# Forming keys already turned, with their norm sent through DRAM, in a fused cross-attention kernel

## The chip, the cores and the metric

The kernel runs on one core of one Trainium2 chip. A core has five engines that run side by side: TensorE (PE; its weight loads are shown apart as PEld), VectorE (DVE), ScalarE (ACT), GpSimd (POOL) and SyncE (SP), which here issues the DMAs. TensorE writes to PSUM (eight banks of 512 float32 for each of 128 partitions); the other engines work on SBUF, and all but GpSimd on PSUM too. The metric is the device time of one execution in microseconds, as the median of several runs.

## What is computed

Eight sequences b of 64 tokens `x[b]` (512 features) attend to a context `ctx[b]` of 1601 rows of 512 features. The part that the change touches is the cross-attention; of the reference:

```python
kvx = jnp.einsum('bsi,oi->bso', cond, w_kv_x)
kx, vx = jnp.split(kvx, 2, axis=-1)
kx = _ln(kx.reshape(b, sc, g, d), kxln_w, kxln_b)      # g = 8 heads of d = 128
vx = vx.reshape(b, sc, g, d)
xout = _gqa(qx, kx, vx).reshape(b, s, nh * d)
...
scores = jnp.einsum('bsghd,btgd->bghst', q, k) * scale
p = jax.nn.softmax(scores, axis=-1)
```

`_ln` subtracts the mean over d, divides by the root of the variance plus 1e-5, then applies a weight and a bias. So each key of each head needs one number of its own, r = 1/sqrt(mean square + 1e-5); the mean is taken out of the weights beforehand (`key_weights`), so that only r is left to find. Around this stand a self-attention with fp8 rounding, an output projection, a sparse attention among the 64 tokens and a ternary feed-forward network. All products with large operands are made exact enough by splitting a float32 number into a high and a low float32r part (`hi`, `lo`) and adding three matmuls: hi x hi, lo x hi, hi x lo.

## The kernel before

**Tiling.** The 1601 context rows are 13 tiles of 128 (`TT`; the last has 65), and the tiles form six chunks (`CHUNKS`): five of 256 keys and one of 321, which is rounded up to 322. The 8 key heads are two halves of 4 (`HG`). There are 16 work items, one for each half and sequence (`Cross`), and so 208 steps of one tile each.

**Order of work.** The loop at the end of `tile_perceiver` runs over g. In each g it issues a piece of several stages at different distances, so that one work item's late stages run beside the next one's early ones: `keys` for tile g (L542), `keys_t` for tile g-1 (L567), `scores` for the chunk that ends at tile g-2 (L580), and, `LAG` = 17 steps behind, `probs_t`, `context` and `weigh` (L621, L653, L678). Everything else (projections, self-attention, feed-forward) comes from generators pumped at a set pace (`bgA`, `bgB`, `bgC`), with lower priority. The program text sets priorities; a scheduler orders each engine's instructions before the run, and on the chip each engine goes through its own in that order.

**Keys.** `keys` loads a tile of the transposed context (cTr, by SyncE, L546), splits it (ScalarE L549 makes cThi, GpSimd L550 makes cTlo), and does 12 matmuls (L555) with the context tile stationary and 512 columns of weights (4 heads) moving, so that the keys lie on partitions. ScalarE squares them into ksq (L560) and copies them to kn (L561), VectorE sums the squares (L562), GpSimd takes the power -1/2 (L173), and VectorE multiplies kn by it (L564). `keys_t` turns kn by four TensorE transposes (L219), and ScalarE (L577, kthi) and VectorE (L578, ktlo) evict the result in two parts.

**Scores.** `scores` does, for each head of a chunk, three matmuls of 256 or 322 columns (L598), two heads in one bank (one head for the last chunk), and VectorE evicts them into the S tile (L602), adding a column of zeros, and takes the maximum on the way. Later ScalarE applies exp (L618), TensorE transposes the probabilities (L630), ScalarE and VectorE split them (L640, L641: phi, plo), and 12 matmuls a tile (L693 to L695) add them up with the context rows (cr, chi, clo) in four banks `acc`.

**Buffers.** S has 7 buffers, cThi and cTlo two each of one tile, raw (cTr, cr and others) three. PSUM: three banks `m` (keys, turned keys, scores, probabilities), four `acc`, one `b`; before step `LAG` - 1 keys use `acc` banks. In the last steps a class `Late` borrows buffers of the main stage for the last token pair.

Of the kernel before, what the change touches and what calls it, by code (L numbers as in the profile page):

```python
# [21 lines left out]
P = 128  # L22
H = 512
NIC = 4
S = 64
# [11 lines left out]
KTW = 324  # L37
NCH = len(CHUNKS)
CHUNK_OF = {tt: ci for ci, ch in enumerate(CHUNKS) for tt in ch}
LAG = 17  # L40
ALL = 10 ** 6
AHEAD = 2000
SPLIT = 1
FFN_AT = 6
# [13 lines left out]
def tile_perceiver(ctx: ExitStack, tc: tile.TileContext, t: dict):  # L58
# [83 lines left out]
    class Late:  # L142
# [5 lines left out]
        def _main(tag, bufs, dt=F32):  # L148
# [6 lines left out]
        pd = _main("kf", 2)  # L155
        ps = staticmethod(lambda tag="b": kxp())

        AT = {"hT": (0, 0), "ps_": (0, 0), "qkv": (0, 256), "sim": (0, 448), "mask": (1, 0), "eq": (1, 64), "cum": (1, 128),
              "pmx": (1, 192), "psu": (1, 224), "aoT": (1, 256), "kvg": (2, 0), "pr": (2, 768), "sT": (2, 1152), "ao": (2, 1216)}

        def tile(self, tag, shape):
            if not self.held:
                self.held = [mp.tile([P, 512], F32, tag="cTlo", name=nm("late"), bufs=2) for _ in range(2)]
                self.held.append(mp.tile([P, HG * KTW], F32, tag="S", name=nm("late"), bufs=7))
            k, o = self.AT[tag]
            a = self.held[k][:shape[0], o:o + math.prod(shape[1:])]
            return a if len(shape) == 2 else a.rearrange("p (x y) -> p x y", x=shape[1])
# [62 lines left out]
    mhalf = ctile([P, 4], F32, "mhalf")  # L230
# [41 lines left out]
    wpd = [dtile([P, 2, H], F32, f"wpd{c}") for c in range(32)]  # L272
    clod = [dtile([SC, H], F32, f"clod{b}") for b in range(NB)]
# [19 lines left out]
    def projection(v_, blocks, js, first=None):  # L293
# [17 lines left out]
        for nb in blocks:  # L311
# [4 lines left out]
            else:  # L316
                ws = [mp.tile([P, NIC, 256], F32, tag="S", name=nm("ws"), bufs=7)]
# [173 lines left out]
    def key_weights(half):  # L491
        hi = mp.tile([P, NIC, 512], F32R, tag="wkhi", name=nm("wkhi"), bufs=1)
        lo = mp.tile([P, NIC, 512], F32R, tag="wklo", name=nm("wklo"), bufs=1)
        for ic in range(NIC):
            tag, bufs = ("kf", 2) if half == 0 and ic >= 2 else ("raw", 3)
# [13 lines left out]
    ksq = ctile([P, HG, D + 1], F32, "ksq")  # L509
    GP.memset(ksq[:, :, D:], EPS)  # L510
# [9 lines left out]
    class Cross:  # L520


        def __init__(self, b, half):
# [4 lines left out]
            self.kn = {}  # L528
# [13 lines left out]
        def keys(self, tt):  # L542

            t0, n = TT[tt]
            raw = mp.tile([P, NIC, P], F32, tag="raw", name=nm("cTr"), bufs=3)
            paced[0] = nc.sync.dma_start(raw[:, :, :n], t["ctxT"][self.b].rearrange("(c p) k -> p c k", p=P)[:, :, t0:t0 + n])  # L546
            chi = mp.tile([P, NIC, P], F32R, tag="cThi", name=nm("cThi"), bufs=2)
            clo = mp.tile([P, NIC, P], F32R, tag="cTlo", name=nm("cTlo"), bufs=2)
            A.copy(chi[:, :, :n], raw[:, :, :n])  # L549
            GP.tensor_tensor(clo[:, :, :n], raw[:, :, :n], chi[:, :, :n].bitcast(F32), ALU.subtract)  # L550
            ps = kxp()
            k = 0
            for st, mv in ((chi, self.wk[0]), (chi, self.wk[1]), (clo, self.wk[0])):
                for ic in range(NIC):
                    PE.matmul(ps[:n], lhsT=st[:, ic, :n], rhs=mv[:, ic, :], start=k == 0, stop=k == 11)  # L555
                    k += 1
            kn = mp.tile([P, 512], F32, tag="kn", name=nm("kn"), bufs=3)
            sq = ksq
            v = sm("kxv", HG)
            A.activation(sq[:n, :, :D], v3(ps[:n], HG), AF.Square, scale=1.0 / math.sqrt(D))  # L560
            A.copy(kn[:n], ps[:n])  # L561
            V.tensor_reduce(v[:n], sq[:n], AX.X, ALU.add)  # L562
            r = rsqrt(v[:n], n, HG, "rqk")
            pin[0] = V.tensor_tensor(v3(kn[:n], HG), v3(kn[:n], HG), r.unsqueeze(2).to_broadcast([n, HG, D]), ALU.mult)  # L564
            self.kn[tt] = kn

        def keys_t(self, tt):  # L567
# [3 lines left out]
            c0 = TT[CHUNKS[ci][0]][0]  # L571
# [584 lines left out]
    for g in range(NA + LAG + 3):  # L1156
# [8 lines left out]
        if g == NA + 3:  # L1165
            lane["late"] = mainp("late")
# [15 lines left out]
        if g < NA:  # L1182
            work[nA].keys(kA)
# [139 lines left out]
```

## Time and profile before

| what | value |
|---|---|
| times of three runs | 1986.89, 1992.36, 1997.09 us |
| median | 1992.36 us |
| span of the profiled execution | 1990.0 us |
| that execution's own time | not given by the profile apart from its span |
| instructions | 32306 |
| DMA traffic | 352.02 MB, mean 177 GB/s |
| DMA queue of SyncE, share of 16 engines | 55.5% |

The span runs from the first to the last instruction of the program in the profiled execution. The profile gives each engine's busy time, then the span in 40 slices, the DMA queues, the chain of work that ended last (followed back from the last instruction to whatever released it), and groups of instructions: line, engine, operation, tiles written and read, shapes, count, then busy us, mean ns of one, the engine's idle time before them, and who ended it. Matmuls overlap in the array, so that one lasts longer than the distance to the next. In the timeline a line is: start, length in us, engine, line, operation, tiles, shape, how many in a row.

### The profile page before, as it was taken

The page shows a single profiled execution, that of the slowest core. Times are in us where ns is not written, and L with a number is a line of the kernel's source. Part 1 is how long each engine was busy: PE and PEld are TensorE (multiplying, and loading weights), DVE is VectorE, ACT ScalarE, POOL GpSimd, SP SyncE. Part 2 cuts the span into 40 slices and gives each one's busy share as a digit, 9 for nine tenths or more (in the row PEclk, how much of TensorE's full clock was granted, in tenths as well). Part 3 has the DMA queues.
Part 4 walks back from the last instruction along what each step waited for, and adds up shares of the span by engine and source line. Part 5 has one row for each costly group of instructions (what it writes and reads, how often), then busy time and mean ns, then how long its engine had stood idle before and what let it go on. Part 6 is the DMA issues. An engine that isn't in the chain of part 4 may idle for free.

```text
span 1990.0 us, 32306 instructions
## 1 busy us (share of the span) xinstructions
PE 1923.4 (97%) x10709; PEld 1593.6 (80%) x10709; DVE 1377.2 (69%) x3423; ACT 1215.9 (61%) x2724; POOL 634.1 (32%) x600
## 2 busy tenths in 40 slices
PE   7899999999999999999999999999999999999998
PEld 5678888888888887887888788888877787886776
DVE  7768688677678676776775665756577665655665
ACT  6576667666676566655664545555675566566554
POOL 6343334333333333223332323222233333220132
PEclk9899999999999999999999999999999999999999
DMA  6345545466455654557776667656745543564425
GB/s 199 115 140 164 160 143 162 142 209 211 132 171 157 216 160 122 186 172 265 236 265 225 200 199 257 200 188 204 269 136 162 172 157 94 156 209 139 142 65 178
DMA packets 296503, 352.02 MB, mean 177 GB/s; under 512 B 30336, under 2 KB 191232, under 8 KB 296336
## 3 DMA queue, kind: packets, MB, share of 16 engines
q1 hardware_dynamic: 296336, 349.97, 55.5%
q8 instruction: 84, 1.38, 0.3%
q14 instruction: 83, 0.68, 0.1%
HBM read 283.94 MB, written 65.68 MB: 176 GB/s over the span
## 4 chain that ended last, share of the span: by engine, by line
PE 83%; DMA 7%; DVE 5%; issue 2%; ACT 1%; POOL 1%; SPq 0%; POOLq 0%; ACTq 0%; DVEq 0%
PE kx L555 26%; PE acc L693 8%; PE acc L694 8%; PE acc L695 8%; PE s L598 6%; PE pj L340 4%; PE pt L630 4%; PE kx L219 4%; DMA ws<-wpd 3%; PE xo L714 3%; PE pp L431 2%; PE p L822 1%; DMA wv<-in_wkv 1%; PE tr L372 1%; PE y L1073 1%
## 5 line engine op out<-in xcount | busy, mean ns | idle before, releaser
L550 POOL TENSOR_TENSOR cTlo<-cTr,cThi 128x512 fp32r<-128x512 f32 (+1 forms) x208 | 274.4, 1320 | 891.2 <-PE kx L555 618.1
L694 PE MATMUL acc<-plo,chi 128*128 128x512 f32 x768 | 310.3, 405 | 0.4 <-DVE plo L641 0.4
L695 PE MATMUL acc<-phi,clo 128*128 128x512 f32 x768 | 303.8, 397 | 0.0
L562 DVE TENSOR_REDUCE kxv<-ksq 128x4 f32<-128x516 f32 (+1 forms) x208 | 142.9, 687 | 223.0 <-ACT ksq L560 222.8
L173 POOL TENSOR_TENSOR rqk<-kxv,mhalf 128x4 f32<-128x4 f32 (+1 forms) x208 | 217.8, 1047 | 127.1 <-DVE kxv L562 109.5
L693 PE MATMUL acc<-phi,chi 128*128 128x512 f32 x768 | 246.7, 402 | 1.7 <-ACT chi L670 1.0
L555 PE MATMUL kx<-wkhi,cThi 128*128 128x512 f32 (+1 forms) x832 | 240.8, 411 | 7.0 <-ACT wkhi L501 2.3
L549 ACT CAST cThi<-cTr 128x512 fp32r<-128x512 f32 (+1 forms) x208 | 125.9, 606 | 182.1 <-PE kx L555 84.1
L555 PE MATMUL kx<-wklo,cThi 128*128 128x512 f32 (+1 forms) x832 | 230.4, 397 | 0.0
L555 PE MATMUL kx<-wkhi,cTlo 128*128 128x512 f32 (+1 forms) x832 | 229.4, 395 | 0.0
L577 ACT ACTIVATE kthi<-kx,cols 128x512 fp32r<-128x512 f32 (+1 forms) x208 | 140.8, 677 | 137.2 <-PE kx L219 135.6
L670 ACT CAST chi<-cr 128x512 fp32r<-128x512 f32 x192 | 119.1, 620 | 141.7 <-PE acc L694 130.5
L618 ACT ACTIVATE S<-S,cnm 128x256 f32<-128x256 f32 (+1 forms) x384 | 197.1, 522 | 7.0 <-DVE cnm L613 6.8
L578 DVE SCALAR_TENSOR_TENSOR ktlo<-kx,cols,kthi 128x512 fp32r<-128x512 f32 (+1 forms) x208 | 150.9, 726 | 60.7 <-ACT kthi L577 59.9
L555 PEld LDWEIGHTS kx<-wklo,cThi 128*128 128x128 f32 (+1 forms) x832 | 155.0, 187 | 41.2 <-issue 1.6
L555 PEld LDWEIGHTS kx<-wkhi,cTlo 128*128 128x128 f32 (+1 forms) x832 | 154.3, 186 | 41.3 <-issue 3.2
L555 PEld LDWEIGHTS kx<-wkhi,cThi 128*128 128x128 f32 (+1 forms) x832 | 147.5, 188 | 39.2 <-ACT wkhi L501 3.5
L564 DVE TENSOR_TENSOR kn<-kn,rqk 128x512 f32<-128x512 f32 (+1 forms) x208 | 149.4, 718 | 39.4 <-POOL rqk L173 36.3
L602 DVE CUSTOM_DVE_ANT_0 S<-s,zeros 128x256 f32<-128x256 f32 (+1 forms) x384 | 151.9, 429 | 33.1 <-PE s L598 32.2
L694 PEld LDWEIGHTS acc<-plo,chi 128*128 128x128 f32 x768 | 145.0, 189 | 26.4 <-issue 1.7
L693 PEld LDWEIGHTS acc<-phi,chi 128*128 128x128 f32 x768 | 139.9, 189 | 32.7 <-ACT chi L670 2.8
L695 PEld LDWEIGHTS acc<-phi,clo 128*128 128x128 f32 x768 | 144.6, 189 | 26.1 <-issue 1.6
(344 smaller groups left out, 3770.5 us busy)
## 6 DMA issues: line engine op xcount, KB each, us to landing
cTr<-in_ctxT SPq DMA_DIRECT2D x192, 256.0 KB
cr<-in_ctx SPq DMA_DIRECT2D x192, 256.0 KB
ws<-wpd SPq DMA_DIRECT2D x88, 512.0 KB
clod<-clo SPq DMA_DIRECT2D x96, 256.0 KB
clo<-clod SPq DMA_DIRECT2D x96, 256.0 KB
wv<-in_wkv SPq DMA_DIRECT2D x64, 256.0 KB
tern<-in_ffn_w SPq DMA_DIRECT2D x64, 256.0 KB
wpd<-ws SPq DMA_DIRECT2D x32, 512.0 KB
```

Source lines behind the costliest of these rows:

```text
L173: GP.tensor_tensor(y[:n], v, mhalf[:n, :k], ALU.pow)
L550: GP.tensor_tensor(clo[:, :, :n], raw[:, :, :n], chi[:, :, :n].bitcast(F32), ALU.subtract)
L555: PE.matmul(ps[:n], lhsT=st[:, ic, :n], rhs=mv[:, ic, :], start=k == 0, stop=k == 11)
L562: V.tensor_reduce(v[:n], sq[:n], AX.X, ALU.add)
L564: pin[0] = V.tensor_tensor(v3(kn[:n], HG), v3(kn[:n], HG), r.unsqueeze(2).to_broadcast([n, HG, D]), ALU.mult)
L577: A.activation(hi[:, :, o], v3(pt, HG)[:, :, :n], AF.Copy, scale=hw["kx"])
L578: V.scalar_tensor_tensor(lo[:, :, o], v3(pt, HG)[:, :, :n], hw["kx"], hi[:, :, o].bitcast(F32), ALU.mult, ALU.subtract)
L602: V.tensor_tensor_reduce(sc[:, g, :cw], ps[:, :cw], zeros.to_broadcast([P, cw]), 1.0, -3.0e38, ALU.add, ALU.max, self.mx[:, g * NCH + ci:g ...
L618: A.activation(self.S[ci][:, g, :cw], self.S[ci][:, g, :cw], AF.Exp, bias=self.nmx[:, g:g + 1], accum_out=self.su[:, g * NCH + ci:g * NCH ...
L693: PE.matmul(self.U[ic], lhsT=chi[:n, s], rhs=phi[:n], start=tt == 0, stop=False)
L694: PE.matmul(self.U[ic], lhsT=chi[:n, s], rhs=plo[:n], start=False, stop=False)
L695: PE.matmul(self.U[ic], lhsT=clo[:n, s], rhs=phi[:n], start=False, stop=False)
```

## The change

Keys are now formed turned: the weights are stationary (128 columns of one head) and a whole chunk of the context moves (256 or 322 columns), so that a head's 128 features lie on partitions and keys along the free dimension, as scores need them. The four transposes of a tile, the copy kn, and the product with r before the transposes are gone. `keys` is split in two: `turned` loads and splits the context of a tile into buffers that hold a chunk (cThi, cTlo: two of 322 columns), and `keys` does two heads of a chunk (one head in the last chunk, whose four heads take three steps), evicting them unnormed.

The norm now runs over partitions. ScalarE's squares are turned by VectorE in 32x32 blocks, and summed over 32 columns (`ms`); `norm`, once a chunk, adds the four blocks of partitions by one TensorE product with a constant (`over`), picks each partition group's own head (`quad`), takes the power on GpSimd, turns the 32x32 blocks once more, writes 128 rows of 32 numbers to DRAM (`keyd`), and reads them back, broadcast to all 128 partitions, into the chunk's S tile. `scores` then multiplies by the S tile where it added zeros.

The stages move: context loads at step g, keys two steps later (`KEYS`), scores four steps after the load (`SCORES`; two before), `LAG` 19. S has 8 buffers (`SB`), taken at `norm`. `Late` moves its borrowed tiles to other tags.

```diff
-LAG = 17
+LAG = 19
+KEYS, SCORES = 2, 4
...
+SB = 8
...
+    quad = ctile([P, HG], F32, "quad")
+    for h in range(HG):
+        V.tensor_reduce(quad[:, h:h + 1], ident[:, h * 32:(h + 1) * 32], AX.X, ALU.add)
+    over = ctile([P, P], F32, "over")
+    for h in range(HG):
+        V.tensor_reduce(over[:, h * 32:(h + 1) * 32], ident.rearrange("p (q a) -> p a q", q=HG), AX.X, ALU.add)
+    spread = [ctile([P, 32], F32, f"spread{i}") for i in range(2)]
...
+    keyd = [[dtile([HG, 1024], F32, f"keyd{i}_{ci}") for ci in range(NCH)] for i in range(2)]
...
-        def keys(self, tt):
+        def turned(self, tt):
 
             t0, n = TT[tt]
+            ci = CHUNK_OF[tt]
+            o = t0 - TT[CHUNKS[ci][0]][0]
+            if ci not in self.ct:
+                self.ct[ci] = [mp.tile([P, NIC, CTW], F32R, tag=x, name=nm(x), bufs=2) for x in ("cThi", "cTlo")]
+            chi, clo = self.ct[ci]
             raw = mp.tile([P, NIC, P], F32, tag="raw", name=nm("cTr"), bufs=3)
...
+            A.copy(chi[:, :, o:o + n], raw[:, :, :n])
+            GP.tensor_tensor(clo[:, :, o:o + n], raw[:, :, :n], chi[:, :, o:o + n].bitcast(F32), ALU.subtract)
+
+        def keys(self, ci, gs):
...
+            ps = kxp()
+            for i, g in enumerate(gs):
+                k = 0
+                for st, mv in ((self.wk[0], chi), (self.wk[1], chi), (self.wk[0], clo)):
+                    for ic in range(NIC):
+                        PE.matmul(ps[:, i * N:(i + 1) * N], lhsT=st[:, ic, g * P:(g + 1) * P], rhs=mv[:, ic, :N], start=k == 0, stop=k == 11)
+                        k += 1
+            g0, g1, ng = gs[0], gs[-1] + 1, len(gs)
+            sq = mp.tile([P, 512], F32, tag="kn", name=nm("ksq"), bufs=3)
...
+            A.activation(v3(sq[:, :ng * W], ng)[:, :, :N], v3(ps[:, :ng * N], ng), AF.Square, scale=1.0 / math.sqrt(D))
+            A.activation(hi[:, g0:g1, :N], v3(ps[:, :ng * N], ng), AF.Copy, scale=hw["kx"])
+            sqt = mp.tile([P, 512], F32, tag="kn", name=nm("ksqt"), bufs=3)
+            V.transpose(sqt[:, :ng * W], sq[:, :ng * W])
+            V.scalar_tensor_tensor(lo[:, g0:g1, :N], v3(ps[:, :ng * N], ng), hw["kx"], hi[:, g0:g1, :N].bitcast(F32), ALU.mult, ALU.subtract)
+            pin[0] = V.tensor_reduce(self.ms[ci][:, g0 * nj:g1 * nj], sqt[:, :ng * W].rearrange("p (x a) -> p x a", a=32), AX.X, ALU.add)
...
+        def norm(self, ci):
+
+            cw = sum(TT[tt][1] for tt in CHUNKS[ci])
+            nj = (cw + 31) // 32
+            ms = self.ms.pop(ci)
+            z = mainp("kz")
+            PE.matmul(z[:, :HG * nj], lhsT=over, rhs=ms[:, :HG * nj], start=True, stop=True)
+            own = sm("kown", HG * NRM, bufs=1)
+            V.scalar_tensor_tensor(v3(own[:, :HG * nj], HG), v3(z[:, :HG * nj], HG), EPS, quad.unsqueeze(2).to_broadcast([P, HG, nj]), ALU.add, ALU.mult)
+            v = sm("kxv", NRM, bufs=2)
+            V.tensor_reduce(v[:, :nj], own[:, :HG * nj].rearrange("p (g j) -> p j g", g=HG), AX.X, ALU.add)
+            r = spread[ci % 2]
+            GP.tensor_tensor(r[:, :nj], v[:, :nj], mhalf[:, :nj], ALU.pow)
+            rt = sm("krt", 32, bufs=2)
+            V.transpose(rt, r)
+            rd = keyd[(self.b + self.half * NB) % 2][ci]
+            nc.sync.dma_start(rd.rearrange("g (x a) -> (g x) a", a=32), rt)
+            self.S[ci] = mp.tile([P, HG, KTW], F32, tag="S", name=nm("S"), bufs=SB)
+            load(self.S[ci][:, :, :cw], rd[:, :cw].partition_broadcast(P))
...
-                    V.tensor_tensor_reduce(sc[:, g, :cw], ps[:, :cw], zeros.to_broadcast([P, cw]), 1.0, -3.0e38,
-                                           ALU.add, ALU.max, self.mx[:, g * NCH + ci:g * NCH + ci + 1])
+                    V.tensor_tensor_reduce(sc[:, g, :cw], ps[:, :cw], sc[:, g, :cw], 1.0, -3.0e38,
+                                           ALU.mult, ALU.max, self.mx[:, g * NCH + ci:g * NCH + ci + 1])
...
+    TURN = {tt: (tt,) for tt in range(NT - 2)}
+    TURN[NT - 2] = NT - 2, NT - 1
+    JOBS = [(ci, [(2 * i, 2 * i + 1)]) for ci in range(NCH - 1) for i in range(2)]
+    JOBS += [(NCH - 1, x) for x in ([(0,)], [(1,)], [(2,), (3,)])]
...
         if g < NA:
-            work[nA].keys(kA)
+            for tt in TURN.get(kA, ()):
+                work[nA].turned(tt)
+        if 0 <= gK < NA:
+            ci, gs = JOBS[kK]
+            for x in gs:
+                work[nK].keys(ci, x)
+            if gs[-1][-1] == HG - 1:
+                work[nK].norm(ci)
...
-        if 0 <= g - 2 < NA:
-            nS, kS = divmod(g - 2, NT)
+        if 0 <= g - SCORES < NA:
+            nS, kS = divmod(g - SCORES, NT)
...
-        if 0 <= g - 1 < NA:
-            nT, kT = divmod(g - 1, NT)
-            work[nT].keys_t(kT)
```

## The prediction

> **What bounds the kernel now.** I read the page first (engines, slices, the chain that ended last), then TensorE in order of time, then the groups by line with shapes kept apart, then the waits. Two lines of the page:
>
> ```profile
> PE 1923.4 (97%) x10709; PEld 1593.6 (80%) x10709; DVE 1377.2 (69%) x3423; ACT 1215.9 (61%) x2724; POOL 634.1 (32%) x600
> ...
> PE kx L555 26%; PE acc L693 8%; PE acc L694 8%; PE acc L695 8%; PE s L598 6%; PE pj L340 4%; PE pt L630 4%; PE kx L219 4%; DMA ws<-wpd 3%; PE xo L714 3%; PE pp L431 2%; PE p L822 1%; DMA wv<-in_wkv 1%; PE tr L372 1%; PE y L1073 1%
> ```
>
> TensorE is busy nearly throughout and the chain's largest items are its matmuls: keys (L555) and key transposes (L219) are the ones that the change rewrites. A matmul's own duration is no price, since matmuls overlap. The price is start to start, which the timeline gives (start, length, instruction):
>
> ```profile
> 51.73 0.60 PE L219 MATMUL kx<-ident,kn 128*128 128x128 f32 x4
> 52.09 1.17 PE L555 MATMUL kx<-wkhi,cThi 128*128 128x512 f32 x4
> 53.09 1.07 PE L555 MATMUL kx<-wklo,cThi 128*128 128x512 f32 x4
> 54.00 1.08 PE L555 MATMUL kx<-wkhi,cTlo 128*128 128x512 f32 x4
> ...
> 73.42 3.00 PE L340 MATMUL pj<-ws,xq 128*128 128x256 f32 x23
> 76.25 1.09 PE L555 MATMUL kx<-wkhi,cThi 128*128 128x512 f32 x4
> ...
> 1026.83 1.09 PE L555 MATMUL kx<-wkhi,cThi 128*128 128x512 f32 x4
> ...
> 1029.56 0.39 PE L693 MATMUL acc<-phi,chi 128*128 128x512 f32 x1
> 1029.79 0.39 PE L598 MATMUL s<-kthi,qxhi 128*128 128x256 f32 x2
> ...
> 1030.49 0.63 PE L693 MATMUL acc<-phi,chi 128*128 128x512 f32 x2
> ```
>
> Read from it: a tile's 12 key matmuls take 1029.56 - 1026.83 = 2.73 us (0.2275 each); six score matmuls of 256 columns, each with weights of its own, take 0.70 (0.117 each); 23 of L340 take 2.83 (0.123). Four transposes take 0.36, and the four matmuls behind them 1.00 instead of 0.91: 0.45 in all.
>
> **TensorE, term by term.** Removed: 192 groups of four transposes x 0.45 = 86.4, and 16 of the one-row-over-64 tile, 0.24 each (1006.59 to 1006.83) = 3.8: **-90.2 us**. Rewritten: 208 x 2.73 = 567.8 becomes, for the 80 chunks of 256 keys, 80 x 48 matmuls of 256 columns, and for the 16 last chunks 16 x 48 of 322 columns. At 0.120, between the two 256-column rows, the first are 460.8 (449.3 at 0.117, 472.3 at 0.123). Three score matmuls of 322 columns start 0.45 apart in sum (1016.28 to 1016.73), so the second are 768 x 0.150 = 115.2. The last chunk gains, since its third tile of 65 keys no longer pays for 512 columns; the rest pays a little. Sum 576.0: **+8.2** (-3.3 to +19.7). Added: 96 small products z of 32 or 44 columns. Nearest: L463, 64 columns, 16 in 1.72 (1022.35 to 1024.07), 0.108 each: **+10.3** (9.6 at the 0.10 of L831's two columns, 22 at the 0.2275 of 512). TensorE together: -71.7.
>
> The Trainium skill speaks against narrower matmuls: "TensorE: Matmul & The Clock Gate", section "LDWEIGHTS (loading the stationary operand)", gives columns / 1.2 ns, so 107 ns for 128 columns whatever the matmul's width, and its section on the gap 256/2.4 + 2.5 = 109 ns; by both, 256 is about the narrowest width that hides the load. By its gap the keys would go from 539 to 524 us (an estimate from that page), -15 where I take +8; the rows above (0.117 to 0.123 and 0.2275) are slower than the page's and decide.
>
> **The other engines.** The groups that lose or change work:
>
> ```profile
> L564 DVE TENSOR_TENSOR kn<-kn,rqk 128x512 f32<-128x512 f32 x192 | 138.6, 722 | 37.1 <-POOL rqk L173 34.0 <-ACT fa L367 2.3
> L562 DVE TENSOR_REDUCE kxv<-ksq 128x4 f32<-128x516 f32 x192 | 132.0, 687 | 213.5 <-ACT ksq L560 213.3
> L602 DVE CUSTOM_DVE_ANT_0 S<-s,zeros 128x256 f32<-128x256 f32 x320 | 121.0, 417 | 15.6 <-PE s L598 14.8
> L561 ACT COPY kn<-kx 128x512 f32<-128x512 f32 x192 | 111.8, 582 | 0.0
> L173 POOL TENSOR_TENSOR rqk<-kxv,mhalf 128x4 f32<-128x4 f32 x192 | 200.5, 1044 | 102.4 <-DVE kxv L562 94.6 <-DVE cqb L605 5.1 <-DVE hag L356 1.0
> ```
>
> VectorE, per 256-key chunk: before 2 x (687 + 722 + 746 of L578) = 4.31 us. After: two turns by 32x32 blocks, two L578-like subtractions, two reductions, and in norm about 0.55 (L364's 217, L610's 160, a small turn). No row shows the turn. Nearest one-input rows of 128x512 are the copy L701 (682) and the reduction (687); I take 690 and keep 290 (L211, the fastest) to 890 (L473, the slowest) as ends. That is 4.8, +0.5 x 80; the last chunk goes from 6.16 to about 7.0, x 16: **+53 us**, 1430 of some 1922, 74%. Evicting scores by a product with the S tile is priced like L602, 417: L1006, also PSUM with SBUF at 256 columns, has 419.
> ScalarE loses 121 us (208 copies) and gains 3 in the last chunk's shapes: 57%. GpSimd loses 217.8; by L173's rows for 1, 2 and 4 columns (607, 700, 1044) a column costs 170 ns, so 80 pows of 8 columns (1.73) and 16 of 11 (2.24) add 174; memsets 10. All of this lies beside TensorE and is priced at nothing. If that cover went, VectorE's 53 is the price (95 with turns of 890, below nothing with turns of 290).
>
> **New waits.** z stands in TensorE's order behind a square, a turn and a reduction; behind it queue acc (L693-695) and scores, and everyone who evicts them. The key transposes waited for such a chain too (copy, reduction, pow, product) and cost 3.8 us of idle in 768; so 0 to 4 us, taken as no change. SyncE gets 192 DMAs: the read into the S tile waits until the write has landed, and for a free S tile (released by pt transposes a step earlier); behind it queue the loads of cTr, cr and clo, the casts, then acc. VectorE's score eviction now waits for that read; behind it queue plo (L641) and again acc. The prices of a trip through DRAM are shown by the DMA queue's waits and the chain in order of time:
>
> ```profile
> SPq L130 <- DMA xrd<-xr: 32.2, 13, 5.8
> ```
>
> ```profile
> 675.17 5.85 DMA ws<-wpd
> ...
> 1131.80 4.95 DMA ws<-wpd
> 1171.38 6.97 DMA ws<-wpd
> ```
>
> A write-then-read waited 32.2/13 = 2.5 us (5.8 at worst); 512 KB, what the broadcast read moves, took 5 to 7 in the load's own traffic; the 256 KB broadcast of L130 between 1873.25 and 1875.05 flowed at 146 GB/s, by which 512 KB are 3.6 us of flow alone. From the last key matmul to a filled S tile: square 0.60, turn 0.69, the subtraction 0.75 that is issued between, reduction 0.69, z 0.27, 0.22 + 0.16 on VectorE, pow 1.73, turn 0.15 = 5.3; about eight hand-overs to busy engines, 0.25 each, 2 (GpSimd's pow may also find a cTlo of 1.37 ahead of it); write 2.5; issue 0.4; read 5 to 7: 15.2 to 17.2 us. The room: keys end in step G, scores come in step G + 2. Loads of cTr run from 4.9 to 1758.6 for 208 steps, 8.47 us a step; less 0.34, two steps are 16.3, plus 0.7 of score matmuls: 17. It fits by 1.8 us or misses by 0.2: priced at 0, since the order of each engine's work leaves a late eviction some other work. DMA queues have room (55% busy; 96 x 512 = 49152 packets of 1 KB and 12288 short ones join 296503).
>
> The start: weighing begins two steps later, in a stretch where TensorE is not full:
>
> ```profile
> 0.00:140.00 140.00, 112.24 (x588) 94.05 (x589) 103.99 (x296) 90.84 (x200) 69.77 (x72) 0.95 0.52 158
> ```
>
> 27.8 us idle over 17 steps, 1.6 a step, two more: **+3.3** (0 to 7).
>
> **Sum.** 1990.0 - 71.7 + 3.3 = 1921.6 for the profiled span. No view shows what lies around the span; the median of the runs, 1992.36, is 2.4 above it, so 1924.
>
> **Rivals.**
> - *The trip through DRAM comes late* (slower). With the worst write (5.8) and read (7) the chain is 20.5, 3.5 beyond the room; VectorE stands still, and after acc's 2.75 us of matmuls TensorE too. From 0.7 us lost per chunk (68.4/96) the gain is gone. Late in half the chunks: 48 x 3.5 = 168, 2092. For it: little room, SyncE's order; against: only the worst rows together reach it, and the casts get a step of lead.
> - *Partly given back*: the turn at 890 or slower, loads delayed behind SyncE's landing waits; a third to two thirds of the gain, 1950 to 1980.
> - *Nothing moves*: stalls of 0.6 to 0.8 a chunk cancel the gain, 1990. TensorE's work shrinks by its own rows, so this needs a coincidence.
> - *Weights don't hide*: if each narrow matmul paid LDWEIGHTS' 190 ns, 160 x 24 x 0.07 + 768 x 0.04 = 300 us, 2225. L598 and L340 have the same shape and don't pay it.
>
> **Chances.** Forecast (1895 to 1950) 0.56; partly given back 0.14; nothing moves 0.08; late trip 0.20; weights 0.02. About 0.5% is what a measurement here can tell from no change. Faster 0.70, same 0.08, slower 0.22. Low end: 1992.4 less 83.9 (the best end of each TensorE term), no start cost, and less the idle that L219, L555 and L598 now have before them (3.8 + 7.0 + 2.9): 1895. High end 2015: half of the late-trip cases lie above.
>
> **What would show it.** Key matmuls of 256 columns 0.117 to 0.123 apart, 322 at 0.150; no L219 kx; VectorE near 74% with turns near 690; no idle before score evictions put down to a DMA; step near 8.1 us. I am wrong if VectorE waits for the DMA into S, if z has idle before it on TensorE, or if the SyncE queue's landing waits exceed 96 x 2.5 us and casts wait for cr.

## The result, and the profile after

The changed kernel takes 2128.26 us (median of four runs, 2126.41 to 2130.39); beside it the kernel before took 1989.62 (1983.02 to 1997.09). The ratio is 1.069, with an interval of 1.066 to 1.072: slower by 139 us, where 68 less were forecast. The profiled execution spans 2127.2 us.

Engines first, from the page of the changed kernel, and the chain that ended last, by engine:

```profile
PE 1919.9 (90%) x12181; PEld 1688.4 (79%) x12181; DVE 1398.5 (66%) x3769; ACT 1105.6 (52%) x2548; POOL 561.8 (26%) x567
...
PE 12%; DVE 2%; DMA 1%; ACT 0%; issue 0%; POOL 0%; SPq 0%; POOLq 0%; DVEq 0%
```

Every engine's share is lower: none has become the bound. The chain's shares add up to a sixth of the span only, so it says nothing on the rest. TensorE's busy time is as before (1923.4), though the transposes are gone. Two more numbers explain that. The stretches in which no matmul ran (worked out from the trace, between the first matmul and the last) add up to 52.0 us before and 193.2 after; 4 of them were over 2 us, now 25. And the mean granted clock (the share of full speed that TensorE's clock was given) went from 0.991 to 0.960, so that the same matmuls take longer.

The key matmuls themselves, in the timeline (start, length, instruction):

```profile
801.95 0.65 PE L586 MATMUL kx<-cThi,wkhi 128*128 128x256 f32 x4
802.43 0.63 PE L586 MATMUL kx<-cThi,wklo 128*128 128x256 f32 x4
802.90 0.64 PE L586 MATMUL kx<-cTlo,wkhi 128*128 128x256 f32 x4
803.38 0.60 PE L671 MATMUL pt<-ident,S 128*128 128x128 f32 x4
...
831.04 0.76 PE L586 MATMUL kx<-cThi,wklo 128*128 128x322 f32 x4
831.64 0.75 PE L586 MATMUL kx<-cTlo,wkhi 128*128 128x322 f32 x4
832.23 0.75 PE L586 MATMUL kx<-cThi,wkhi 128*128 128x322 f32 x4
```

Twelve of 256 columns take 803.38 - 801.95 = 1.43 us, 0.119 each; eight of 322 take 832.23 - 831.04 = 1.19, 0.149 each. Both are the forecast's prices. The new operations of the other engines (mean in ns, and the engine's idle time before them):

```profile
L614 POOL TENSOR_TENSOR spread<-kxv,mhalf 128x8 f32<-128x8 f32 x80 | 135.9, 1699 | 164.1 <-DVE kxv L612 154.4 <-PE kx L586 5.7 <-PE s L639 3.8
L643 DVE CUSTOM_DVE_ANT_0 S<-s,S 128x256 f32<-128x256 f32 x320 | 119.8, 418 | 54.2 <-DMA S<-keyd 27.5 <-PE s L639 17.8 <-PE acc L736 4.1
...
L596 DVE STREAM_TRANSPOSE ksqt<-ksq 128x512 f32<-128x512 f32 x160 | 113.2, 708 | 157.1 <-ACT ksq L593 156.6
```

A turn takes 708 ns (690 was taken), a power 1699 (1730), an eviction 418 (417). So durations were right; what was lost is in the waits (us in all, times, longest):

```profile
ACT cThi L567 <- DMA cTr<-in_ctxT: 185.4, 84, 8.9
...
DVE S L643 <- DMA S<-keyd: 37.2, 19, 3.8
...
PE kz L608 <- DVE kms L598: 28.9, 22, 3.6
...
PE pp L444 <- DMA ws<-wpd: 24.9, 16, 4.1
```

```profile
SPq L134 <- DMA keyd<-krt: 176.0, 86, 6.2
...
SPq L618 <- DVE krt L616: 65.4, 42, 3.9
```

Two lines of the kernel before, the key transposes' idle and the casts' wait for context, stand beside them:

```profile
L219 PE MATMUL kx<-ident,kn 128*128 128x128 f32 x768 | 116.0, 273 | 3.8 <-DVE ktlo L578 1.6 <-ACT kn L561 1.2 <-DVE kn L564 1.0
```

```profile
ACT cThi L549 <- DMA cTr<-in_ctxT: 32.0, 24, 3.8
```

The score evictions wait rarely for the S tile (19 of 384). TensorE waits 22 times for z's sums; before, the key transposes lost 3.8 us behind their chain. SyncE's queue stands 65 us until the numbers to write are there (krt) and 176 us for the write to land. None of these is 139 us long and on TensorE, so the waits alone don't tell what the time went into; that needed the experiments.

One of z's waits, in TensorE's timeline (in brackets the idle time before, and who ended it) and, after it, in VectorE's:

```profile
283.56 0.39 PE L736 MATMUL acc<-phi,clo 128*128 128x512 f32 x1
287.57 0.64 PE L608 MATMUL kz<-kms,over 128*128 128x32 f32 x2 [3.62 <-DVE kms L598]
288.02 0.77 PE L639 MATMUL s<-kthi,qxhi 128*128 128x256 f32 x2
288.59 0.63 PE L639 MATMUL s<-kthi,qxlo 128*128 128x256 f32 x2
...
292.59 0.65 PE L586 MATMUL kx<-cThi,wklo 128*128 128x256 f32 x4
```

```profile
282.89 1.65 DVE L340 SCALAR_TENSOR_TENSOR ws<-ld,cols,ws 128x256 fp32r<-128x256 f32 x2
284.46 0.21 DVE L372 TENSOR_SCALAR hv<-hag,wsc 128x4 f32<-128x4 f32 x1
284.60 0.47 DVE L340 SCALAR_TENSOR_TENSOR ws<-ld,cols,ws 128x256 fp32r<-128x256 f32 x1
284.99 0.69 DVE L596 STREAM_TRANSPOSE ksqt<-ksq 128x512 f32<-128x512 f32 x1
285.62 0.70 DVE L597 SCALAR_TENSOR_TENSOR ktlo<-kx,cols,kthi 128x512 fp32r<-128x512 f32 x1
286.25 0.67 DVE L715 TENSOR_TENSOR clo<-cr,chi 128x512 fp32r<-128x512 f32 x1
286.85 0.67 DVE L598 TENSOR_REDUCE kms<-ksqt 128x16 f32<-128x512 f32 x1
```

ScalarE's square had ended at 283.31. The turn starts 1.7 us later, behind a projection's weights (L340), and between turn and reduction VectorE does 1.37 us of other work. TensorE has scores to do, which start as soon as z is through, and key matmuls, but z stands ahead of them. What follows is the second price, seen in windows of that stretch (the third number from the right is the granted clock):

```profile
283.00:288.00 5.00, 1.38 (x7) 0.88 (x6) 4.81 (x10) 1.54 (x4) 2.03 (x2) 0.95 0.71 222
288.00:292.00 4.00, 4.00 (x25) 4.00 (x26) 2.39 (x12) 1.51 (x5) 1.64 (x1) 0.64 0.41 121
292.00:296.00 4.00, 4.00 (x36) 4.00 (x35) 3.04 (x8) 3.18 (x9) 0.00 (x0) 1.00 0.39 123
```

After 3.62 us without a matmul the clock is granted at 0.64 over the next four microseconds, which hold 25 matmuls; the four after those hold 36. The Trainium skill, "TensorE: Matmul & The Clock Gate", section "Part 1: The HAM clock gate (the "warmup" mystery)", says that the array falls to half its clock after an idle window of about 3.4 us and needs about as long a busy one to come back. The stretch above agrees.

### The profile page after: what moved, and what is told of

Read it like the earlier page. It is cut to its first block, busy times and chain, and to the rows that moved or that the text cites. A ratio compares the mean times of both kernels' runs of the same rounds, so it can differ in the third digit from the quotient of the medians.

```text
span 2127.2 us, 36082 instructions
## 1 busy us (share of the span) xinstructions
PE 1919.9 (90%) x12181; PEld 1688.4 (79%) x12181; DVE 1398.5 (66%) x3769; ACT 1105.6 (52%) x2548; POOL 561.8 (26%) x567
## 5 line engine op out<-in xcount | busy, mean ns | idle before, releaser
L586 PE MATMUL kx<-cThi,wkhi 128*128 128x256 f32 (+1 forms) x1536 | 281.4, 304 | 15.5 <-DVE cmx L643 9.5
L596 DVE STREAM_TRANSPOSE ksqt<-ksq 128x512 f32<-128x512 f32 (+1 forms) x224 | 147.7, 659 | 192.9 <-ACT ksq L593 191.1
L567 ACT CAST cThi<-cTr 128x512 fp32r<-128x512 f32 (+1 forms) x208 | 124.1, 606 | 285.7 <-DMA cTr<-in_ctxT 185.4
L586 PE MATMUL kx<-cTlo,wkhi 128*128 128x256 f32 (+1 forms) x1536 | 266.9, 293 | 0.0
L586 PE MATMUL kx<-cThi,wklo 128*128 128x256 f32 (+1 forms) x1536 | 265.0, 293 | 0.0
L586 PEld LDWEIGHTS kx<-cThi,wkhi 128*128 128x128 f32 x1536 | 229.0, 197 | 33.5 <-DVE cmx L643 14.8
L586 PEld LDWEIGHTS kx<-cTlo,wkhi 128*128 128x128 f32 x1536 | 225.0, 194 | 4.0 <-issue 2.4
L586 PEld LDWEIGHTS kx<-cThi,wklo 128*128 128x128 f32 x1536 | 225.2, 195 | 1.8 <-issue 0.8
L614 POOL TENSOR_TENSOR spread<-kxv,mhalf 128x8 f32<-128x8 f32 x96 | 170.3, 1774 | 181.1 <-DVE kxv L612 171.4
L643 DVE CUSTOM_DVE_ANT_0 S<-s,S 128x256 f32<-128x256 f32 (+1 forms) x384 | 150.6, 429 | 70.4 <-DMA S<-keyd 37.2
L682 DVE TENSOR_TENSOR plo<-pt,phi 128x512 fp32r<-128x512 f32 x192 | 131.2, 684 | 62.4 <-ACT phi L681 61.6
```

The costliest lines, as they stand in the source:

```text
L567: A.copy(chi[:, :, o:o + n], raw[:, :, :n])
L586: PE.matmul(ps[:, i * N:(i + 1) * N], lhsT=st[:, ic, g * P:(g + 1) * P], rhs=mv[:, ic, :N], start=k == 0, stop=k == 11)
L596: V.transpose(sqt[:, :ng * W], sq[:, :ng * W])
L614: GP.tensor_tensor(r[:, :nj], v[:, :nj], mhalf[:, :nj], ALU.pow)
L643: V.tensor_tensor_reduce(sc[:, g, :cw], ps[:, :cw], sc[:, g, :cw], 1.0, -3.0e38, ALU.mult, ALU.max, self.mx[:, g * NCH + ci:g * NCH + ci + 1])
L682: V.tensor_tensor(lo[:n], pt[:n], hi[:n].bitcast(F32), ALU.subtract)
```

## The experiments

**The theories.** *Z*: the product z stands in TensorE's order behind ScalarE and VectorE, and what it loses there is most of the time. *Q*: SyncE stands for the landing of the write, and loads behind it come late. *C*: the context's casts, ahead of other work on ScalarE, pass late loads on. *The named rival*: score evictions wait for the read.

All results, ordered; the kernel before took 1989.62 to 1995.21 (medians) beside them. The last two columns are of the profiled execution: time without a matmul, as above, and stretches of it over 2 us.

| kernel | us (median) | ratio to before, interval | no matmul, us | over 2 us |
|---|---|---|---|---|
| turned keys only, no norm | 1908.19 | 0.958 (0.951 to 0.966) | 68.9 | 5 |
| no trip, z multiplies a constant | 1953.26 | 0.980 (0.977 to 0.982) | 76.1 | 6 |
| no trip, norm a step later | 1953.96 | 0.980 (0.976 to 0.984) | 81.4 | 6 |
| squares, turns and sums only | 1957.90 | 0.983 (0.974 to 0.992) | 99.9 | 9 |
| no trip | 2023.63 | 1.016 (1.013 to 1.019) | 130.2 | 9 |
| z multiplies a constant | 2053.72 | 1.031 (1.023 to 1.040) | 146.1 | 21 |
| fixed read, no write | 2065.37 | 1.037 (1.032 to 1.043) | 150.6 | 15 |
| ScalarE's queue, cast late | 2069.96 | 1.038 (1.033 to 1.043) | 150.8 | 18 |
| trip on ScalarE's queue | 2085.58 | 1.047 (1.040 to 1.054) | 167.0 | 20 |
| write, read of 4 KB | 2087.70 | 1.047 (1.043 to 1.051) | 167.3 | 17 |
| cast late | 2098.77 | 1.054 (1.051 to 1.057) | 168.8 | 26 |
| **the changed kernel** | **2128.26** | **1.069 (1.066 to 1.072)** | **193.2** | **25** |
| trip on GpSimd's queue | 2130.61 | 1.070 (1.063 to 1.077) | 194.7 | 24 |
| read a step later | 2137.77 | 1.073 (1.070 to 1.076) | 196.9 | 31 |
| norm later, ScalarE's queue | 2153.77 | 1.083 (1.079 to 1.086) | 203.1 | 22 |
| norm a step later | 2161.21 | 1.085 (1.082 to 1.088) | 218.1 | 24 |
| norm later, ScalarE's queue, cast late | 2202.06 | 1.106 (1.103 to 1.109) | 247.7 | 37 |
| before with LAG 19 | 2211.07 | 1.110 (1.105 to 1.115) | 197.5 | 15 |
| norm by ones, logarithm and exp | 2216.93 | 1.113 (1.109 to 1.116) | 235.2 | 32 |

### What each part costs

**Turned keys only.** `norm` keeps only the S tile, `scores` adds zeros as before, and `keys` loses:

```diff
-            A.activation(v3(sq[:, :ng * W], ng)[:, :, :N], v3(ps[:, :ng * N], ng), AF.Square, scale=1.0 / math.sqrt(D))
...
-            V.transpose(sqt[:, :ng * W], sq[:, :ng * W])
...
-            pin[0] = V.tensor_reduce(self.ms[ci][:, g0 * nj:g1 * nj], sqt[:, :ng * W].rearrange("p (x a) -> p x a", a=32), AX.X, ALU.add)
```

> Left out: the whole norm (squares, their turns and sums, the product z, power, write and read); keys are formed turned and split, scores are not normed. This is the change on TensorE alone. My forecast's terms for TensorE without z: 1990 - 82 + 3 = about 1911 if nothing else stands in the way. Theory Q or Z: 1900 to 1930. Theory C: the casts are still exposed, 2000 to 2080.

1908: TensorE's terms hold in sum. The forecast without z's 10.3 is 1924 - 10 = 1914. The parts are less exact, and cancel by luck: in the profiled execution matmuls last 94 us less than before (1923.4 to 1829.0), where the terms without z say 82, and 17 us more pass without one (52.0 to 68.9), where the start term says 3.3. The casts still waited 170.8 us for context here (87 times) without harm, which speaks against theory C.

**Squares, turns and sums, unused.**

```diff
         def norm(self, ci):
...
-            ms = self.ms.pop(ci)
-            z = mainp("kz")
...
+            self.ms.pop(ci)
...
-            load(self.S[ci][:, :, :cw], rd[:, :cw].partition_broadcast(P))
```

> Left out: everything of the norm behind the sums (product z, its eviction, power, turn, write, read); the squares, the 32x32 turns and the sums are made and not used, scores are evicted by adding zeros, not normed. It parts the 116 us between the run without the trip (2024) and the run with keys turned alone (1908). Theory Z (TensorE's in-order wait at z and what it drags along): 1915 to 1945. Theory B (a key bank is released late, since its eviction on VectorE now stands behind a turn and before a sum, and VectorE is at 70% again): 1980 to 2015.

1958, between the two theories' ranges, and 50 us more than without them (39 to 61 between single runs), though VectorE is far from full. The prediction had named 53 as the price if the cover were gone; that this is near is chance, since its 53 are VectorE's growth over the kernel before, while VectorE's busy time grows by 230 us between these two kernels (1116.3 to 1346.6).

**No trip.** All of norm up to the second turn; no write, no read.

```diff
-            nc.sync.dma_start(rd.rearrange("g (x a) -> (g x) a", a=32), rt)
...
-            load(self.S[ci][:, :, :cw], rd[:, :cw].partition_broadcast(P))
...
-                    V.tensor_tensor_reduce(sc[:, g, :cw], ps[:, :cw], sc[:, g, :cw], 1.0, -3.0e38,
-                                           ALU.mult, ALU.max, self.mx[:, g * NCH + ci:g * NCH + ci + 1])
+                    V.tensor_tensor_reduce(sc[:, g, :cw], ps[:, :cw], zeros.to_broadcast([P, cw]), 1.0, -3.0e38,
+                                           ALU.add, ALU.max, self.mx[:, g * NCH + ci:g * NCH + ci + 1])
```

> Left out: the write of r and its broadcast read; scores are evicted by adding zeros as before the change, so they are not normed. Theory Q: as in the run with the fixed read or lower, 1960 to 2030, since SyncE also loses the waits for a free S tile and the DMA engines lose 52 MB. Theory C: context loads find emptier queues, 2060 to 2110. Theory Z: 2090 to 2120.

2024: z, power and second turn cost 66 us over the last kernel, the trip 105 of the rest.

**Fixed read**: the S tile is read from a piece of DRAM written once, so that no read waits for a write.

```diff
+    nc.sync.dma_start(fixd.rearrange("g (x a) -> (g x) a", a=32), ones[:, :32])
...
-            nc.sync.dma_start(rd.rearrange("g (x a) -> (g x) a", a=32), rt)
...
-            load(self.S[ci][:, :, :cw], rd[:, :cw].partition_broadcast(P))
+            load(self.S[ci][:, :, :cw], fixd[:, :cw].partition_broadcast(P))
```

> Left out: the per-chunk write of r to DRAM; the S tile is filled from one DRAM tile written once at the start, so the scores are not normed. The norm's product, power and turns still run, the 96 broadcast reads still move 512 KB each. Theory Q (SyncE stands still 176 us for the landing of 86 writes, and the context loads behind it come late): most of the 138 us goes, 1990 to 2040. Theory C (context casts on ScalarE now run as soon as their load is due and hold ScalarE until it lands, whatever SyncE does): 2090 to 2125. Theory Z (TensorE stands at the small product of the norm): 2090 to 2125.

**Write, and a read of 4 KB** into a small tile instead of the S tile.

```diff
-            load(self.S[ci][:, :, :cw], rd[:, :cw].partition_broadcast(P))
+            self.row[ci] = small.tile([P, HG, 2], F32, tag="row", name=nm("row"), bufs=3)
+            load(self.row[ci], rd[:, :2].partition_broadcast(P))
```

> The write and the wait for its landing stay; the read after it is cut to two numbers of each head for each partition (4 KB instead of 512 KB), into a small tile of its own instead of the S tile, and scores multiply by one of them (the norm is thus wrong for most keys). If the 512 KB and the wait for a free S tile are the price of the trip: 2025 to 2050. If it is SyncE's standing for the write's landing and the order around it: 2085 to 2115.

The fixed read's 2065 lies between the ranges of its theories; 2024 and 2088 each lie within one. With neither write nor full read 2024, with the read alone 2065 (+42), with write and landing wait alone 2088 (+64), with both 2128 (+105). The two prices add within a microsecond or two. In the kernel with the short read SyncE stood 154.2 us in 82 waits for the landing and 84.0 in 48 for the numbers to write, and 9 score evictions waited 26.7 us for the short read; no run parts the 64 among them. The 42 are bytes, the wait for a free S tile, or both; no run here parts these either.

### z's place

**z multiplies a constant**, in the changed kernel and in the one without a trip:

```diff
-            PE.matmul(z[:, :HG * nj], lhsT=over, rhs=ms[:, :HG * nj], start=True, stop=True)
+            PE.matmul(z[:, :HG * nj], lhsT=over, rhs=ident[:, :HG * nj], start=True, stop=True)
```

> The changed kernel, but the product z multiplies a constant instead of the sums, so it waits for nothing on VectorE; the norm's value is wrong, the rest of the chain, the write and the read stay, and the sums are made and not used. Theory Z: 60 to 110 us below the changed kernel, 2020 to 2070. Theory B: only z's own idle (31 us), 2090 to 2115.

> No trip through DRAM (no write, no read; scores add zeros, so keys stay unnormed), and z multiplies a constant instead of the sums, so it has nothing to wait for; squares, 32x32 turns, sums, the power and the small turn are all still done. With z's wait the same kernel took 2024, without z and power 1958. If z's wait on TensorE is what costs 66 us: 1960 to 1980. If it is the bank that z holds, or the small operations on VectorE and GpSimd: 2005 to 2025.

75 us go in the complete kernel (theory Z's range), 70 in the one without a trip (7 below the range that was expected for z's wait), and in the latter only 45 are left over turned keys alone, the price of squares, turns and sums. So z's product, its bank, and the work of the small operations and the power cost nothing that shows; its wait does. Compare the pages of the kernels without a trip, first with z on a constant, then with z on the sums:

```profile
PE 1858.7 (95%) x12181; PEld 1652.5 (85%) x12181; DVE 1387.9 (71%) x3769; ACT 1100.7 (56%) x2548; POOL 564.4 (29%) x567
```

```profile
PE 1878.5 (93%) x12181; PEld 1655.6 (82%) x12181; DVE 1396.4 (69%) x3769; ACT 1105.8 (55%) x2548; POOL 561.2 (28%) x567
```

The same 12181 matmuls last 20 us longer, and 54 us more pass without one (130.2 - 76.1): 74, the difference of the spans. z's own listed waits in the second are 17.8 us in 17 waits; the rest is probably what came late behind it, which no view adds up.

**Norm a step later**, behind the next chunk's first key matmuls; scores a step later too and ahead of keys in the step, LAG 20; first complete, then without the trip.

```diff
-KEYS, SCORES = 2, 4
+KEYS, SCORES = 2, 5
...
-            if gs[-1][-1] == HG - 1:
-                work[nK].norm(ci)
+        if 0 <= gK - 1 < NA:
+            nN, kN = divmod(gK - 1, NT)
+            if JOBS[kN][1][-1][-1] == HG - 1:
+                work[nN].norm(JOBS[kN][0])
```

> The complete computation. The whole of norm (product z, power, turn, write, read) is issued one step later, behind the first matmuls of the next chunk's keys, and scores one step later too (SCORES 5, LAG 20), so that the trip has as much room as before. If TensorE's wait at z for the sums is the largest price in place (75 us went when z multiplied a constant), 2045 to 2070, with less than 10 us of waits of kz for kms. If the price of z was its place among the PSUM banks and not the wait, 2110 to 2130.

> As the kernel with norm one step later, without the trip (no write, no read; scores add zeros, keys stay unnormed). z waits for the true sums but comes behind the next chunk's first key matmuls. If the late z is as good as one that needn't wait, 1950 to 1975 (1953 with z on a constant, 2024 with z in its old place). If the order of that kernel, with scores ahead of keys and a step later, costs by itself: 2000 to 2040, and then the late reads were not the whole loss of that kernel.

Without the trip the late z is as good as a constant one: 1954 against 1953, with the true sums, for which z waits once, 0.9 us. This also settles a rival. VectorE, too, stands behind z, for its product (kown): 54.4 us with z in its old place without the trip, but 74.8 with the late z, which is 70 us faster. So the price goes with TensorE's wait, not with VectorE's. With the trip it is 2161, a miss on both expectations. The waits of that kernel tell why:

```profile
DVE S L643 <- DMA S<-keyd: 291.9, 84, 10.9
...
PE s L639 <- DVE cqb L646: 25.4, 13, 4.3
...
PE kz L608 <- DVE kms L598: 3.9, 1, 3.9
```

z waits for its sums once. Instead VectorE waits 84 times for the read, 3.5 us each. The expectation that the trip has as much room as before was wrong. Where there is no trip to wait for, the first score eviction of a chunk comes 17.5 us behind z's start (median) in the changed kernel's order, and 9.2 in this one, since scores now stand ahead of keys in the step. The shortest of these distances with a trip is 10.7 us here, the median 14.5 (19.0 in the changed kernel). So the named rival is real, but in the changed kernel it was mostly out of reach. The whole trip costs 2161 - 1954 = 207 us here; SyncE still stands 106.8 us for its landing, so not all of that is late reads.

### The trip's queue

**Write and read on another queue**: GpSimd's, then ScalarE's (`nc.scalar` instead of `nc.gpsimd`).

```diff
-            nc.sync.dma_start(rd.rearrange("g (x a) -> (g x) a", a=32), rt)
+            nc.gpsimd.dma_start(rd.rearrange("g (x a) -> (g x) a", a=32), rt)
...
-            load(self.S[ci][:, :, :cw], rd[:, :cw].partition_broadcast(P))
+            nc.gpsimd.dma_start(self.S[ci][:, :, :cw], rd[:, :cw].partition_broadcast(P))
```

> The changed kernel whole; the write of r and its broadcast read are issued by GpSimd instead of SyncE, so that GpSimd waits for the landing. Theory Q (63 us of the loss are SyncE standing still): 2050 to 2085, GpSimd's cTlo later. If GpSimd's waits do the same harm or its DMAs are slower: 2110 to 2180.

> The same with ScalarE as the issuer, which then waits for each landing (some 3 us, 96 times, 13% of its time). Theory Q: SyncE is free, but ScalarE evicts keys and probabilities, so the gain is lost again: 2100 to 2250. Were SyncE's queue the only harm, as with GpSimd: 2050 to 2085.

ScalarE's queue saves 43 us, GpSimd's none. There the wait only moved, in front of the power and cTlo:

```profile
POOL S L620 <- DMA keyd<-krt: 168.4, 63, 5.7
```

On ScalarE's queue the listed waits for the landing add up to 56 us only, against 176 on SyncE's. Theory Q as stated missed in both: with SyncE free it expected 2050 to 2085 on GpSimd's queue and 2100 to 2250 on ScalarE's. What the runs show is narrower: the trip costs as much where GpSimd stands 168 us for the landing as where SyncE stands 176, and 43 less where ScalarE stands 56. So the price goes with how long the issuing engine stands, whichever it is; that it comes from loads late behind SyncE is argued, not shown. Why ScalarE's landing waits are short stays open.

**The read issued a step later**, with the later scores and the order of the kernel with norm a step later.

```diff
+        if 0 <= gK - 1 < NA:
+            nN, kN = divmod(gK - 1, NT)
+            if JOBS[kN][1][-1][-1] == HG - 1:
+                work[nN].scale(JOBS[kN][0])
```

> The complete computation. The write to DRAM stays where it is, but the broadcast read into the S tile is issued one step later, and scores and everything behind them come one step later too (SCORES 5, LAG 20). The product z stays in its place. If SyncE's standing for the write's landing is what cost about 60 us (2128 against 2065 where the read had nothing to wait for), most of it goes: 2065 to 2085. If it is z's wait on TensorE alone that holds the kernel, nothing goes but the few score evictions that met a late read: 2105 to 2130. No expectation is below 2050.

2138, and no test of Q: SyncE still stood 169.8 us in 83 waits, since its order put the read soon behind the write again. It shows that the later scores and the later read, with z in its old place, together cost little (10 us).

### The casts, and all together

**Cast late**: the context's cast is issued behind the previous step's key eviction (`evicted`, the copy into kthi).

```diff
-            A.copy(chi[:, :, o:o + n], raw[:, :, :n])
+            with tc.issue_after(evicted[0].ins) if evicted[0] is not None else nullcontext():
+                A.copy(chi[:, :, o:o + n], raw[:, :, :n])
```

> The changed kernel whole, but the context cast of a step is placed on ScalarE behind the eviction of the keys of the step before. Theory C: the loads get a step of lead again, ScalarE's wait for them (185 us) falls below 60 and the time to 2030 to 2080. Theory Q: SyncE's landing waits stay, 2110 to 2140. Theory Z: 2110 to 2140.

**The gains together**: ScalarE's queue and the late cast; norm a step later with ScalarE's queue; all three.

> The complete computation with the changed kernel's order: the write and the read go through ScalarE's queue (alone 43 us off), and the context's cast is issued behind the previous step's key eviction (alone 30 off). If the two prices add: 2045 to 2065. If the cast only suffered from loads behind SyncE's wait: 2080 to 2095, as with ScalarE's queue alone.

> As the kernel with norm one step later, and the write and the read go through ScalarE's queue instead of SyncE's (alone that took 43 us away). If the two prices add: 75 + 43 off 2128, so 2000 to 2030. If they are one and the same lost time counted twice, 2045 to 2070, the same as norm one step later alone.

> As the last, and the context's cast is issued behind the previous step's key eviction on ScalarE (alone that took 30 us away). If all three add: 1970 to 2005, about the kernel before (1990). If the cast's place only mattered while loads came late behind SyncE's wait, 2000 to 2030 as without it.

Of these four kernels none met an expectation; the first came 19 us above theory C's range. The late cast gives 30 alone and 16 on top of ScalarE's queue: 2070 is the fastest complete version of turned keys that was run, still slower than before. With norm a step later nothing adds, since score evictions keep waiting for the read (261.0 us in 78 waits with ScalarE's queue), and the late cast then makes it worse by 48. Theory C is no main cause: with the late cast alone the casts' wait for context falls from 185.4 to 7.0 us, further than C asked, and the time by 30 only. Nor are the 30 all C's, for z's waits fall as well, from 28.9 to 4.8 us. That z hardly waits there and the kernel still takes 2099 is an open end; what the late cast costs elsewhere isn't shown.

### The start, and another norm

**The kernel before with LAG 19**, nothing else.

```diff
-LAG = 17
+LAG = 19
```

> The kernel before with LAG 19 instead of 17 and nothing else. By the prediction's start term, 3.3 us (0 to 7) more than before: 1990 to 1997. If the first steps are worth a step's whole idle of the changed kernel's start, 10 to 20 more: 2003 to 2013.

216 us more, far outside both expectations. It didn't isolate the start. Among its waits are two that the kernel before doesn't list (VectorE's score evictions waited for score matmuls alone there):

```profile
PE pt L630 <- DVE ktlo L578: 58.0, 46, 3.2
...
DVE S L602 <- PE pt L630: 27.1, 34, 1.6
```

A score eviction now waits until transposes have freed an S tile. Probably the seven S tiles, held two steps longer, are too few, as the changed kernel's eighth suggests; the run doesn't prove it. The start is read from the windows instead. In the first 140 us TensorE is busy for (changed kernel, then turned keys only; before 112.24):

```profile
0.00:140.00 140.00, 89.38 (x612) 82.63 (x612) 99.51 (x315) 71.26 (x156) 56.30 (x63) 0.89 0.58 173
```

```profile
0.00:140.00 140.00, 99.41 (x690) 93.68 (x690) 81.65 (x273) 71.24 (x161) 47.01 (x54) 0.91 0.51 152
```

**The norm by a matrix of ones**, a logarithm and exp on ScalarE, without turns or DRAM.

```diff
+                PE.matmul(z[:, :ng * N], lhsT=onesr, rhs=sq[:, :ng * N], start=True, stop=True)
+                A.activation(self.S[ci][:, g0:g1, :cw], v3(z[:, :ng * N], ng)[:, :, :cw], AF.Ln, bias=epsc)
+                A.activation(self.S[ci][:, g0:g1, :cw], self.S[ci][:, g0:g1, :cw], AF.Exp, scale=-0.5)
```

> Keys formed turned, the norm in another way: one product of the squares with a matrix of ones, a step after the keys, leaves each key's mean square on all 128 partitions; ScalarE takes the logarithm and then exp of -1/2 of it, into the S tile. No turns, no sums, no power, no DRAM; the squares are rounded to float32r. TensorE gets 160 products of 512 columns and 64 of 322 (about 47 us at 0.2275 and 0.15), ScalarE 448 operations and table loads for the logarithm (about 290 us, 66 per cent busy). If the lost time is the chain of small hand-overs: 1908 + 47 and little else, 1950 to 1985. If TensorE waits for ScalarE's two operations and table loads in the place of DRAM: 2010 to 2060.

2217, outside both. ScalarE became busy for 84%; the page of its groups shows what the expectation missed:

```profile
L611 ACT ACT_TABLE_LOAD x208 | 266.9, 1283 | 3.7
L612 ACT ACT_TABLE_LOAD x167 | 214.3, 1283 | 3.0
```

Of the 224 logarithms (L611) 208 have a table load of their own, of the 224 exps behind them (L612) 167: 375 loads, 481 us.

## Why the prediction was wrong

The gain on TensorE was forecast rightly in sum; what failed are three terms that were put at nothing.

- **TensorE's terms: right in sum.** 0.119 and 0.149 a key matmul, 1908 for turned keys alone against 1914 by the forecast's terms, with two misses of 12 to 14 us that cancel. z's 10.3 us don't show (1953 with it and 1958 without).
- **"All of this lies beside TensorE and is priced at nothing": wrong by 50 us** (1908 to 1958). The durations were right, and VectorE's busy time grew by less than forecast (21 us instead of 53). But ScalarE and VectorE work in order, and what TensorE needs from them (banks evicted, splits done) probably comes later behind a turn and a reduction.
- **The step that failed: "so 0 to 4 us, taken as no change"** for z. It measures 66 to 75 us (2024 against 1958, 1954 or 1953; 2128 against 2054). The comparison with the key transposes was wrong: by the text of the kernel before, those of tile g-1 were issued beside the key matmuls of tile g, a step behind their chain, while z's chain ends with the same step's squares. z moved by a step measures as free, in the kernel without a trip.
- **The trip through DRAM, "priced at 0": 105 us**, 64 for the write and what waits for it, 42 for the read. The forecast asked whether the trip fits between keys and scores, and mostly it does (19 late evictions of 384). Much of the price goes with the issuing queue: 176.0 us in 86 waits is 2.05 us a wait, near the 2.5 that the prediction took. It named the loads and casts queued behind, but priced only the S tile that waits. Its sign for this, landing waits over 96 x 2.5 = 240 us, never came; the other two signs of being wrong, idle before z and VectorE waiting for the S tile, did. (The Trainium skill, "DMA: Bandwidth & Descriptors", section "Anatomy of one DMA — SWDGE (gpsimd) path", gives about 2.0 us fixed for a DMA from GpSimd; here 2.05 is a mean wait on SyncE's queue.)
- **The start, +3.3:** 140 - 89.38 is 50.6 us not busy, against 27.8: 22.8 more. But 12.8 of these are there with turned keys alone as well, whose total was on forecast, so this is no clear part of the loss.
- **The rival on the slower side** had the right sign and a real mechanism, but not this kernel's. It named late reads; 37 us of them occurred.

The sum: 1924 forecast, less 16 (turned keys were 6 below their terms, and z's 10 isn't seen), + 50 + 66 + 64 + 42 = 2130 against 2128. The first of these terms are differences between runs in a row and meet by construction; the test in it is that 64 and 42, each measured alone, give the 105 of both. Against the kernel without a trip and z on a constant, the changed one has 117 us more without a matmul (193.2 - 76.1) and 61 us more of matmul time for the same matmuls (1919.9 - 1858.7); together the 178 by which the spans differ. The granted clocks agree: 0.040 of 2127.2 us were lost in the one and 0.013 of 1949.1 in the other, 85 and 25 us, 60 apart. So each microsecond of idle brought about half a microsecond of slower matmuls with it; between the two kernels without a trip it was 20 us for 54.

How the 50 us of squares, turns and sums split between later banks and changed order of the engines stays open, and so does the split of the trip's 64; each edit also lets the scheduler order the engines anew.

## What to carry to other kernels

A small product whose operand comes from other engines belongs a full stage behind the work that makes it: here the same product cost 70 us in the stage that made its sums and nothing one stage later. When a step is moved, the room behind it moves as well: the trip through DRAM cost 105 us where scores came 17.5 us behind z without it, and 207 where they came 9.2 behind. A read that must wait for a write's landing is also priced by what stands behind it on the engine that issues it: SyncE's and GpSimd's queues cost the same here, ScalarE's 43 us less.

## What the hardware showed unexpectedly

Idle time on TensorE was paid 1.4 to 1.5 times: 117 us without matmuls came with 61 us of slower ones, 54 with 20. A single pause of 3.62 us left the clock at 0.64 over the next four microseconds. Logarithm and exp in turn on ScalarE cost 375 table loads of 1.283 us, 481 of its 1864.6 busy us in that kernel.
